# Selective scan: a second image by columns, whole products with C, sums two groups behind, softplus' parts added on TensorE, 11 of 32 products with B on GpSimd

## The chip, the cores and the metric

The kernel runs on one core of a Trainium2 chip. A core has five engines that run side by side and meet through semaphores: TensorE (PE in the profile: matmul), VectorE (DVE), ScalarE (ACT), GpSimd (POOL) and SyncE (SP, which issues most DMA here). SBUF is the working memory of 128 partitions, PSUM the memory that TensorE writes. The metric is the device time of one execution in microseconds, from the first to the last instruction and what lies around them; smaller is better.

## The reference

Four layers follow each other on an image of 2 x 128 channels x 64 x 64: attention (layer 0), a block with deformable convolutions (1), six 3 x 3 convolutions (2), and a selective scan in four directions (3). Only layer 3 is concerned:

```
x_norm = layernorm(x over channels);  x_norm_t = x_norm by columns
mamba(s):                                   # s: 4096 tokens of 128 channels, d_inner = 256
    xh, z = split(s @ W_in.T);  xh = silu(causal_conv4(xh) + conv_b)
    dt, B, C = split(xh @ W_xp.T)           # 8, 16, 16
    dt = softplus(dt @ W_dt.T + b_dt)
    dA = exp(dt * A);  dBu = dt * B * xh    # each 4096 x 256 x 16
    h_t = dA_t * h_(t-1) + dBu_t            # the scan
    y = sum_n h_t[n] * C_t[n] + xh * D;  return (y * silu(z)) @ W_out.T
out = x + fuse(mamba(x_norm), flip(mamba(flip)), and the same two of x_norm_t) + b_fuse
```

## The kernel before, in words

**Blocks, groups, slots.** Layer 3 walks through 64 blocks: two images, four directions (rows, columns, columns reversed, rows reversed), eight pieces of 512 tokens. A block has two halves of 128 inner channels, and a half has four groups of four states each (`NJ = 4`). A group is a tile `db` of 128 x 4 x 512: partition 32 j + c holds state j of the group and channel c, and the four columns q = 0..3 are the four sets of 32 channels. So a block has eight groups, called slots 0 to 7 here: slots 0 to 3 are the first half, 4 to 7 the second. Group k of the whole walk is slot k % 8 of block k // 8.

**A group's work.** `weights` spreads the group's four rows of B over the partitions with one matmul into PSUM (`pb`, two buffers of pool `psb`). `db_dve` (L1379) multiplies three of the four columns by B on VectorE, from PSUM; `db_pool` (L1386) does the fourth on GpSimd from a copy of B that DMA has spread in SBUF (`copies`). `expo` (L1393) makes exp(dt A) on ScalarE into one of three PSUM buffers. `scan` (L1402) runs the recurrence in place on VectorE, one column at a time. `keep` copies the last state, for two columns at a time, on ScalarE. `cmul` (L1413) multiplies by C in place on GpSimd, two columns at a time. `sums` (L1419, L1421) adds the states up on TensorE into `py`, of which there is one buffer; the first group of a half adds the D term first. After four groups `gate` (L1430) multiplies `py` by silu(z) on VectorE. `db` has four buffers.

**A block's preparation** goes on one block ahead, a piece in each slot: convolution (`conv`, one half in slot 6 and one in 7 of the block before), `conv_silu` in slot 0, the projections to dt, B and C (`xproj`, slot 1), `delta` and `softplus` (slots 2 and 3), the rest of B and C to full precision (`xproj_rest`, slot 4), silu(z) (slot 5). `softplus` is Relu(v) + ln(1 + exp(-|v|)); `spread` adds the parts and multiplies by u on GpSimd in slots 3 and 4, and the result goes to DRAM and back to have its channels spread over the partitions (`spread_store`, `spread_load`, on SP's queue). The finished block is projected (`project`, slot 3) and added to the image (`finish`, slot 4). The small PSUM tiles of all this share two buffers of pool `psm`.

**The order** is written out by hand: under `tc.manual_schedule()` each engine runs its instructions in program order, and a scheduler changes nothing. The loop over k runs, for each group: transfers, `weights(k+2)`, four times (an exponential two scans ahead, a scan), `db_dve(k+1)`, `db_pool(k+1)`, the products with C, the slot's piece of preparation, and `sums(k-1)` last. A step of iteration k on TensorE thus stands behind `weights(k+2)`, whose buffer is free when `db_dve(k)` has read it.

**Columns.** One normed image `xn` per image of the batch, by rows. The column directions read it with a stride (`window`), three halo rows on each side written by GpSimd. LN of image 1 runs during blocks 22 to 29, with its mean and variance in pool `psm`.

Of the kernel before, what the change touches and what calls it, by code (L numbers as in the profile page):

```python
# [10 lines left out]
F32 = mybir.dt.float32  # L11
# [1109 lines left out]
def layer3(g, I, out):  # L1121
# [7 lines left out]
    ND = 3  # L1129
    NNG = N_STATE // NJ  # L1130
    HB = 3
    with ExitStack() as ctx:
# [9 lines left out]
        wxp = a.tile([P, 2, 40], F32, name="wxp")  # L1142
        nc.sync.dma_start(wxp, I["wxpT"])
        wdt = a.tile([40, 2, P], F32, name="wdt")
        nc.sync.dma_start(wdt[32:40], I["wdtT"])
# [54 lines left out]
        xns = [a.tile([P, HW + 2 * HB, HW], F32, name=f"xn{b}") for b in range(NB)]  # L1200
# [3 lines left out]
        def ln_mean(b, k):  # L1204
            N[k, "mean"] = psm.tile([P, BLK], F32, name="pm3")
            nc.tensor.matmul(N[k, "mean"], onesm, interior(g, b, k * RB, RB), start=True, stop=True)
# [13 lines left out]
        def ln_var(b, k):  # L1220
            N[k, "var"] = psm.tile([P, BLK], F32, name="pm3")
            nc.tensor.matmul(N[k, "var"], onesm, N[k, "sq"], start=True, stop=True)
# [6 lines left out]

        def ln_store(b, k):  # L1230
            xn = xns[b]
            nc.scalar.activation(
                flat(xn[:, HB + k * RB : HB + (k + 1) * RB, :]), N[k, "xc"], AF.Identity, bias=vec(g, "ln_b"), scale=vec(g, "ln_w")
            )

        def columns_halo(b):

            xn = xns[b]
            top, bot = xn[:, 0:HB, :], xn[:, HB + HW :, :]
            nc.gpsimd.tensor_copy(top[:, :, 1:], xn[:, HW : HW + HB, : HW - 1])  # L1240
            nc.gpsimd.memset(top[:, :, 0:1], 0.0)
            nc.gpsimd.tensor_copy(bot[:, :, : HW - 1], xn[:, HB : 2 * HB, 1:])
            nc.gpsimd.memset(bot[:, :, HW - 1 :], 0.0)

        def rows_halo(b):
            nc.gpsimd.memset(xns[b][:, HB - 1, HW - HB :], 0.0)
            nc.gpsimd.memset(xns[b][:, HB + HW, :HB], 0.0)


        dirs = ((0, False, False), (2, True, False), (3, True, True), (1, False, True))  # L1250
# [4 lines left out]
            for c in (range(NBLK - 1, -1, -1) if dirs[nd][2] else range(NBLK))  # L1255
        ]
        NBK = len(blocks)
        S = {}

        def window(blk, shift):  # L1260

            b, nd, c = blk
            xn = xns[b]
            if dirs[nd][1]:
                r0 = HB - shift
                return xn[:, r0 : r0 + HW, c * RB : (c + 1) * RB].rearrange("p h w -> p w h")
            f0 = HB * HW + c * BLK - shift
            return flat(xn)[:, f0 : f0 + BLK]

        def shaped(blk, t):  # L1270

            return img(t) if dirs[blk[1]][1] else t

        def conv(i, hf):
            blk = blocks[i]
            sgn = -1 if dirs[blk[1]][2] else 1
            pu = S[i]["pu", hf] = psm.tile([P, BLK], F32, name="pm3")
            for s in range(4):
                nc.tensor.matmul(shaped(blk, pu), wcs[:, hf, s, :], window(blk, sgn * s), start=(s == 0), stop=(s == 3))  # L1279
# [7 lines left out]
        def zproj(i):  # L1287
            S[i]["pz"] = []
            for hf in range(2):
                pz = psm.tile([P, BLK], F32, name="pm3")  # L1290
                nc.tensor.matmul(shaped(blocks[i], pz), winz[:, hf, :], window(blocks[i], 0), start=True, stop=True)
# [8 lines left out]
        def xproj(i):  # L1300
            S[i]["px"] = px = psm.tile([P, BLK], F32, name="pm3")
            for hf in range(2):
                nc.tensor.matmul(px[:40, :], wxp[:, hf, :], S[i]["u"][:, hf, :], start=(hf == 0), stop=(hf == 1))

        def xproj_copy(i):

            px = S[i].pop("px")
            S[i]["xd"] = ck.tile([40, BLK], F32, name="xd", bufs=1)
            nc.scalar.copy(S[i]["xd"], px[:40, :])
# [17 lines left out]
        def delta(i, hf):  # L1327
            pdt = S[i]["pdt", hf] = psm.tile([P, BLK], F32, name="pm3")
            nc.tensor.matmul(pdt, wdt[32:40, hf, :], S[i]["xd"][32:40], start=True, stop=True)
# [9 lines left out]

        def spread(i, hf):  # L1340
            s_ = S[i]
            dd = s_["dd", hf]
            nc.gpsimd.tensor_add(dd[:, 0, :], dd[:, 0, :], dd[:, 1, :])
# [24 lines left out]
        def copies(i, x, ng):  # L1368

            t = S[i][x, ng] = ck.tile([P, BLK], F32, name=f"{x}4_{ng}", bufs=1)  # L1370
# [4 lines left out]
        def db_dve(k):  # L1375
            i, hf, ng = groups[k]
            x, n = G[k], ND
# [5 lines left out]
        def db_pool(k):  # L1383
            i, hf, ng = groups[k]
            x, n = G[k], ND
# [10 lines left out]
        def scan(k, q):  # L1396
            i, hf, ng = groups[k]
            d0, d1 = G[k].pop(("da", q)), G[k]["db"][:, q, :]
            if dirs[blocks[i][1]][2]:
# [4 lines left out]
        def keep(k, h):  # L1404
            i, hf, ng = groups[k]
            last = 0 if dirs[blocks[i][1]][2] else BLK - 1
            qs = slice(2 * h, 2 * h + 2)
            nc.scalar.copy(hl[:, hf, ng, qs], G[k]["db"][:, qs, last : last + 1])  # L1408

        def cmul(k, h):  # L1410
            i, hf, ng = groups[k]
            v = G[k]["db"][:, 2 * h : 2 * h + 2, :]
            nc.gpsimd.tensor_mul(v, v, S[i]["c", ng].unsqueeze(1).to_broadcast([P, 2, BLK]))  # L1413
# [18 lines left out]
        def project(i):  # L1432
# [4 lines left out]
            s_["xv"] = columns(g, b, c * RB, RB) if dirs[nd][1] else interior(g, b, c * RB, RB)  # L1437
            nc.tensor.matmul(img(pf), g.ident, s_["xv"], start=True, stop=False)
            for hf in range(2):
                nc.tensor.matmul(pf, mt[:, hf, dirs[nd][0], :], s_["gt", hf], start=False, stop=(hf == 1))  # L1440
# [16 lines left out]
        def begin(i):  # L1457
            if i < NBK:
                S[i] = {}
                if i % (4 * NBLK) in (0, 3 * NBLK):  # L1460
                    rows_halo(blocks[i][0])
                if i % (4 * NBLK) == NBLK:
                    columns_halo(blocks[i][0])
# [4 lines left out]
        def front_act(i, slot):  # L1468
            if i < NBK:
                if slot == 0:  # L1470
                    conv_silu(i)
                elif slot == 1:
                    xproj_copy(i)
                elif slot == 2:
                    softplus(i, 0)
                elif slot == 3:
                    softplus(i, 1)
                elif slot == 4:
                    rest_copy(i)
                elif slot == 5:  # L1480
                    zproj_silu(i)


        def transfers(i, slot):
            if i < NBK:
                if slot == 2:
# [13 lines left out]
        def front_pe(i, slot):  # L1500
            if i < NBK:
                if slot == 1:
# [267 lines left out]
```

## Time and profile before

| what | before |
|---|---|
| time, median of 3 runs | 5972.63 us (5970.81 to 5975.61) |
| the profiled execution's own time | 5970.06 us |
| its span, first to last instruction | 5968.2 us |
| first and last scan of layer 3 | about 2518 and 5955 us |
| VectorE, busy in the whole span | 4554.8 us (76%) |
| GpSimd | 3699.7 us (62%) |
| ScalarE | 3806.8 us (64%) |
| TensorE, matmul | 5213.9 us (87%) |
| mean granted TensorE clock | 0.899 |

The whole-span shares are means over stages. In the second half of the span, where the scan is, VectorE and GpSimd each show nine tenths or more in almost every slice. A matmul of 32-bit numbers shows as two instructions ("passes"), so the counts of TensorE's rows are twice those of the code. A matmul's duration in the profile is longer than its distance to the next one, since they are pipelined. "L1402" is line 1402 of the kernel before; "<-" in square brackets names what ended an engine's wait.

### The profile page before, as it was taken

How to read it: one execution, taken by the hardware profiler on the slowest of the kernel's cores; microseconds unless marked ns; L12 is line 12 of the kernel's file. 1: busy time of each engine (PE TensorE's matmuls, PEld its weight loads, DVE VectorE, ACT ScalarE, POOL GpSimd, SP SyncE). 2: the span in 40 equal slices, each digit the busy share in tenths (PEclk: the TensorE clock that was granted, in tenths of full speed). 3: DMA queues.
4: the chain of work that ended last, by engine and by line, in shares of the span. 5: the costliest groups of instructions: out<-in, count | busy, mean ns of one | idle time of the engine just before them, and what ended most of it. 6: DMA issues, size and time to landing. Idle time of an engine off the chain costs nothing.

```text
span 5968.2 us, 60083 instructions
## 1 busy us (share of the span) xinstructions
PE 5213.9 (87%) x18726; PEld 1661.8 (28%) x18726; DVE 4554.8 (76%) x4262; ACT 3806.8 (64%) x5867; POOL 3699.7 (62%) x2112
## 2 busy tenths in 40 slices
PE   7999999989978689877888988788878889888777
PEld 3333333334444234222222222222222222222221
DVE  5333333364134688599999999999999999999999
ACT  4888888830035411477777777777666777777765
POOL 5111111100010121299999999999999999999998
PEclk8999999999989899888888898878888898988887
DMA  5000001030066100255556555555566555655564
GB/s 153 18 18 18 19 18 33 1 58 1 15 117 114 46 4 0 55 144 133 136 135 149 139 137 132 141 138 134 144 146 145 133 137 133 150 140 135 134 147 106
DMA packets 357689, 575.61 MB, mean 96 GB/s; under 512 B 74696, under 2 KB 129360, under 8 KB 356272
## 3 DMA queue, kind: packets, MB, share of 16 engines
q1 hardware_dynamic: 354224, 568.13, 40.1%
q10 hardware_dynamic: 3136, 3.56, 0.2%
q8 instruction: 149, 2.44, 0.2%
q14 instruction: 180, 1.47, 0.1%
HBM read 482.34 MB, written 89.13 MB: 96 GB/s over the span
## 4 chain that ended last, share of the span: by engine, by line
DVE 46%; PE 39%; DMA 5%; issue 4%; POOL 3%; ACT 2%; SPq 1%; DVEq 0%; ACTq 0%; POOLq 0%
DVE db L1402 31%; DVE db L1379 11%; PE ps L287 10%; PE acc L303 8%; PE m L1052 5%; PE m L566 5%; PE acd L812 2%; DMA dd<-dx 2%; POOL db L1413 1%; PE m L526 1%; DVE gt L1430 1%; DMA b<-bx 1%; PE pf L775 1%; PE pm L1279 1%; PE py L1421 1%
## 5 line engine op out<-in xcount | busy, mean ns | idle before, releaser
L1413 POOL TENSOR_TENSOR db<-db,c 128x1024 f32<-128x1024 f32 x1024 | 2400.1, 2359 | 82.4 <-ACT hl L1408 72.8
L1402 DVE TENSOR_TENSOR_SCAN db<-da,hl,db 128x512 f32<-128x512 f32 x1792 | 2158.3, 1265 | 52.2 <-ACT da L1393 5.2
L1393 ACT ACTIVATE da<-dd,am 128x512 f32<-128x512 f32 x2048 | 1406.9, 689 | 901.9 <-DVE db L1402 895.1
L293 ACT ACTIVATE e<-ps 128x1024 f16<-128x1024 f32 x1024 | 992.2, 1021 | 134.6 <-PE ps L287 116.9
L1421 PE MATMUL py<-db,fold 128*32 128x512 f32 x4096 | 825.4, 680 | 195.9 <-POOL db L1413 195.6
L1379 DVE TENSOR_TENSOR db<-pbc,dd 128x1536 f32<-128x1536 f32 x512 | 889.0, 1736 | 1.8 <-DMA c<-bx 1.8
L1279 PE MATMUL pm<-xn,wcs 128*128 128x512 f32 x1024 | 723.1, 857 | 32.4 <-DVE xc L1217 19.3
L314 DVE RECIPROCAL rec<-acc 32x512 f32<-32x512 f32 x64 | 214.9, 3358 | 639.2 <-PE acc L303 612.0
L321 POOL TENSOR_TENSOR parts<-parts 32x512 f32<-32x512 f32 x64 | 80.4, 1256 | 975.1 <-DVE parts L320 975.1
L287 PE MATMUL ps<-q,k 32*128 32x512 f32 x4096 | 656.3, 643 | 3.5 <-DVE flag L250 2.7
L1386 POOL TENSOR_TENSOR db<-b,dd 128x512 f32<-128x512 f32 x512 | 650.9, 1271 | 4.2 <-DMA b<-bx 2.3
L303 PE MATMUL acc<-e,v 128*128 128x512 f16 x2048 | 531.4, 382 | 0.0
L1052 PE MATMUL m<-v,u 128*128 128x512 f32 x864 | 379.6, 603 | 49.4 <-DVE v L1021 49.4
L1419 PE MATMUL py<-u,ddp 128*128 128x512 f32 x256 | 178.1, 784 | 228.2 <-DVE gt L1430 227.9
L1365 PE MATMUL pbc<-bc,sel 64*128 64x512 f32 x512 | 283.9, 555 | 87.5 <-DVE db L1379 83.1
L1421 PEld LDWEIGHTS py<-db,fold 128*32 128x32 f32 x4096 | 115.2, 113 | 798.5 <-POOL db L1413 501.3
L1279 PEld LDWEIGHTS pm<-xn,wcs 128*128 128x128 f32 x1024 | 202.4, 209 | 426.9 <-issue 371.3
L1402 DVE TENSOR_TENSOR_SCAN db<-da,db 128x512 f32<-128x512 f32 x256 | 293.4, 1205 | 17.8 <-ACT da L1393 10.4
L303 PEld LDWEIGHTS <-v 128*128 128x128 bf16 x2048 | 158.4, 97 | 509.8 <-issue 388.4
L287 PEld LDWEIGHTS ps<-q,k 32*128 32x128 f32 x4096 | 229.6, 184 | 227.9 <-issue 145.1
L1365 PEld LDWEIGHTS pbc<-bc,sel 64*128 64x128 f32 x512 | 104.6, 204 | 603.9 <-DVE db L1379 310.1
L566 PE MATMUL m<-comb,w 64*128 64x512 f32 (+4 forms) x1296 | 269.9, 575 | 0.0
(311 smaller groups left out, 5734.7 us busy)
## 6 DMA issues: line engine op xcount, KB each, us to landing
dd<-dx SPq DMA_DIRECT2D x1024, 256.0 KB, 6.5
dx<-dd SPq DMA_DIRECT2D x128, 512.0 KB, 7.3
b<-bx SPq DMA_DIRECT2D x1024, 64.0 KB, 5.2
c<-bx SPq DMA_DIRECT2D x1024, 64.0 KB, 2.0
hats<-pos SPq DMA_DIRECT2D x136, 256.0 KB, 9.6
q<-qd SPq DMA_DIRECT2D x32, 512.0 KB, 8.4
w<-in_conv0T SPq DMA_DIRECT2D x18, 288.0 KB, 8.7
q<-in_x SPq DMA_DIRECT2D x8, 512.0 KB, 7.2
```

What stands on the lines that cost most here:

```text
L287: nc.tensor.matmul(ps[:, i, :], k4[h % 2][rows, kb // 4, :], q4[h % 2][rows, qb * BLK : (qb + 1) * BLK], start=True, stop=True,)
L293: nc.scalar.activation(e[:, :n, :], ps[:, :n, :], AF.Exp)
L303: nc.tensor.matmul(acc, v3[b][:, kb, h, :], e[:, i, :], start=(kb == 0), stop=(kb == NS - 1))
L566: yield lambda q=q, dy=dy, src=src, i0=i0, i1=i1: nc.tensor.matmul(m[:, i0 * NF : i1 * NF], w[half, dy, q, x, :], src, start=(dy == KC and ...
L1052: nc.tensor.matmul(m[x], weights[j][:, dy, x, :], v[j][b][:, x, r0 : r0 + RP, :].rearrange("p r i -> p (r i)"), start=(dy == 0), stop=(dy ...
L1279: nc.tensor.matmul(shaped(blk, pu), wcs[:, hf, s, :], window(blk, sgn * s), start=(s == 0), stop=(s == 3))
L1379: nc.vector.tensor_tensor(x["db"][:, :n, :], x.pop("pb").unsqueeze(1).to_broadcast([P, n, BLK]), S[i]["d4", hf][:, 1, :n, :], ALU.mult)
L1386: nc.gpsimd.tensor_tensor(x["db"][:, n:, :], S[i]["b", ng].unsqueeze(1).to_broadcast([P, 4 - n, BLK]), S[i]["d4", hf][:, 1, n:, :], ALU.mult)
L1393: nc.scalar.activation(da, S[i]["d4", hf][:, 0, q, :], AF.Exp, scale=am[:, hf, q, ng : ng + 1])
L1402: nc.vector.tensor_tensor_scan(d1, d0, d1, 0.0 if first else hl[:, hf, ng, q, :], ALU.mult, ALU.add)
L1413: nc.gpsimd.tensor_mul(v, v, S[i]["c", ng].unsqueeze(1).to_broadcast([P, 2, BLK]))
L1421: nc.tensor.matmul(S[i]["y", hf][32 * q : 32 * q + 32, :], fold, G[k]["db"][:, q, :], start=False, stop=(ng == NNG - 1),)
```

## The change

Seven edits in layer 3, with the sizes of PSUM and of `db` as before:

- Products with B: a table `ND[half][group]` says how many of the four columns VectorE does: 2, 4, 1, 4 in the first half and 1, 4, 1, 4 in the second. GpSimd does the rest, 11 of 32 (8 before). Groups with 4 need no copy of B by DMA.
- Products with C and the state copies are whole: one GpSimd instruction and one ScalarE instruction of four columns a group.
- `sums` runs for the group two behind, not one behind. The gates move from slots 5 and 1 (after the fourth scan) to slots 6 and 2 (after the second scan).
- The parts of softplus are added by TensorE (two matmuls with the identity) and copied back by ScalarE; GpSimd only multiplies. The weights for dt are laid out twice, so that both halves' `delta` stand in one slot.
- The preparation moves about one slot forward; `project` and `finish` stand in slot 5, with the first half's convolution behind them, and the second half's in slot 6; `conv_silu` is in slot 7.
- The image lies twice in SBUF: `xn` by rows and `xt` by columns, each serving both images of the batch. `turn` makes one from the other on ScalarE in slot 6 of a few blocks. Image 1 starts with the columns. The halo rows and their GpSimd copies go.
- LN takes its two PSUM tiles from pool `psb`, the one of `weights`, and runs in slots 0, 1, 3, 4 and 5 of blocks 22 to 29.

```diff
-    ND = 3
+    ND = ((2, 4, 1, 4), (1, 4, 1, 4))
...
-    HB = 3
+    HB = 1
+    HC = 3
...
-        wxp = a.tile([P, 2, 40], F32, name="wxp")
+        wxp = a.tile([P, 2, 72], F32, name="wxp")
...
-        xns = [a.tile([P, HW + 2 * HB, HW], F32, name=f"xn{b}") for b in range(NB)]
+        xn = a.tile([P, HW + 2 * HB, HW], F32, name="xn")
+        xt = a.tile([P, L + 2 * HC], F32, name="xt")
...
-            N[k, "mean"] = psm.tile([P, BLK], F32, name="pm3")
+            N[k, "mean"] = psb.tile([P, BLK], F32, name="pbc")
...
-            N[k, "var"] = psm.tile([P, BLK], F32, name="pm3")
+            N[k, "var"] = psb.tile([P, BLK], F32, name="pbc")
...
+        def turn(b, k):
+            if b:
+                nc.scalar.copy(by_row(k), by_column(k))
+            else:
+                nc.scalar.copy(by_column(k), by_row(k))
...
+        dirs = (
+            ((0, False, False), (2, True, False), (3, True, True), (1, False, True)),
+            ((2, True, False), (3, True, True), (0, False, False), (1, False, True)),
+        )
...
-            if dirs[nd][1]:
-                r0 = HB - shift
-                return xn[:, r0 : r0 + HW, c * RB : (c + 1) * RB].rearrange("p h w -> p w h")
-            f0 = HB * HW + c * BLK - shift
-            return flat(xn)[:, f0 : f0 + BLK]
+            f0 = c * BLK - shift
+            if dirs[b][nd][1]:
+                return xt[:, HC + f0 : HC + f0 + BLK]
+            return flat(xn)[:, HB * HW + f0 : HB * HW + f0 + BLK]
...
+        def sum_parts(i, hf):
+            ps = S[i]["dt", hf] = psm.tile([P, BLK], F32, name="pm3")
+            for x in range(2):
+                nc.tensor.matmul(ps, g.ident, S[i]["dd", hf][:, x, :], start=(x == 0), stop=(x == 1))
+
+        def sum_copy(i, hf):
+            nc.scalar.copy(S[i]["dd", hf][:, 0, :], S[i].pop(("dt", hf)))
...
-            nc.gpsimd.tensor_add(dd[:, 0, :], dd[:, 0, :], dd[:, 1, :])
...
+            if x == "b" and ND[0][ng] == ND[1][ng] == 4:
+                return
...
-            x, n = G[k], ND
+            x, n = G[k], ND[hf][ng]
...
-            nc.scalar.copy(hl[:, hf, ng, qs], G[k]["db"][:, qs, last : last + 1])
+            nc.scalar.copy(hl[:, hf, ng], G[k]["db"][:, :, last : last + 1])
...
-            v = G[k]["db"][:, 2 * h : 2 * h + 2, :]
-            nc.gpsimd.tensor_mul(v, v, S[i]["c", ng].unsqueeze(1).to_broadcast([P, 2, BLK]))
+            v = G[k]["db"]
+            nc.gpsimd.tensor_mul(v, v, S[i]["c", ng].unsqueeze(1).to_broadcast([P, 4, BLK]))
...
                 if slot == 0:
-                    conv_silu(i)
+                    xproj_copy(i)
                 elif slot == 1:
-                    xproj_copy(i)
+                    softplus(i, 0)
                 elif slot == 2:
-                    softplus(i, 0)
+                    softplus(i, 1)
+                    sum_copy(i, 0)
                 elif slot == 3:
-                    softplus(i, 1)
+                    sum_copy(i, 1)
+                    rest_copy(i)
                 elif slot == 4:
-                    rest_copy(i)
-                elif slot == 5:
                     zproj_silu(i)
+            if i + 1 < NBK and slot == 7:
+                conv_silu(i + 1)
...
-                if slot == 2:
+                if slot == 1:
                     bc_store(i)
...
-                if slot == 1:
+                if slot == 0:
                     xproj(i)
+                elif slot == 1:
+                    delta(i, 0)
+                    delta(i, 1)
                 elif slot == 2:
-                    delta(i, 0)
+                    sum_parts(i, 0)
                 elif slot == 3:
-                    delta(i, 1)
+                    sum_parts(i, 1)
+                    xproj_rest(i)
                 elif slot == 4:
-                    xproj_rest(i)
-                elif slot == 5:
                     zproj(i)
             if i + 1 < NBK:
-                if slot == 6:
+                if slot == 5:
                     begin(i + 1)
-                elif slot == 7:
+                elif slot == 6:
                     conv(i + 1, 1)
...
-        LN = {6: ln_mean, 7: ln_square, 8: ln_var, 9: ln_scale, 10: ln_store}
+        LN = {0: ln_mean, 1: ln_square, 3: ln_var, 4: ln_scale, 5: ln_store}
...
-                    for j, hf in (((k - 5) // 8, 0), ((k - 9) // 8, 1)):
-                        if q == 3 and 8 * j + 5 + 4 * hf == k and 0 <= j < NBK:
+                    for j, hf in (((k - 6) // 8, 0), ((k - 10) // 8, 1)):
+                        if q == 1 and 8 * j + 6 + 4 * hf == k and 0 <= j < NBK:
                             gate(j, hf)
-
-                    if q == 2 and live:
-                        keep(k, 0)
                 if more:
                     db_dve(k + 1)
                     db_pool(k + 1)
                 if ended:
-                    cmul(k - 1, 1)
+                    cmul(k - 1)
+                if i >= 1 and i <= NBK:
+                    if slot == 5:
+                        project(i - 1)
+                        finish(i - 1)
                 front_pe(i + 1, slot)
                 front_act(i + 1, slot)
                 front_pool(i + 1, slot)
-                if i >= 1 and i <= NBK:
-                    if slot == 3:
-                        project(i - 1)
-                    elif slot == 4:
-                        finish(i - 1)
                 if live:
                     next_norm(i, slot)
-                if live:
-                    cmul(k, 0)
-                if ended:
-                    sums(k - 1)
+
+                    if slot == 6 and i % (4 * NBLK) < NBLK // 2:
+                        for n in range(2):
+                            turn(blocks[i][0], 2 * (i % (4 * NBLK)) + n)
+
+                if 0 <= k - 2 < len(groups):
+                    sums(k - 2)
```

## The prediction

> **What bounds the kernel now.** I read the page's busy table and slices, then layer 3 (the scan, the only part that changes) by stretches, by groups and in order of time. Four rows of the costliest groups carry the stage:
>
> ```profile
> L1413 POOL TENSOR_TENSOR db<-db,c 128x1024 f32<-128x1024 f32 x1024 | 2400.1, 2359 | 82.4 <-ACT hl L1408 72.8
> L1402 DVE TENSOR_TENSOR_SCAN db<-da,hl,db 128x512 f32<-128x512 f32 x1792 | 2158.3, 1265 | 52.2 <-ACT da L1393 5.2
> ...
> L1379 DVE TENSOR_TENSOR db<-pbc,dd 128x1536 f32<-128x1536 f32 x512 | 889.0, 1736 | 1.8 <-DMA c<-bx 1.8
> ...
> L1386 POOL TENSOR_TENSOR db<-b,dd 128x512 f32<-128x512 f32 x512 | 650.9, 1271 | 4.2 <-DMA b<-bx 2.3
> ```
>
> Busy time by stretches (eight blocks in this row; columns: length, then PE, PEld, DVE, ACT, POOL, granted clock, DMA share, GB/s):
>
> ```profile
> 4235.00:4664.00 429.00, 351.55 (x918) 92.38 (x917) 420.84 (x337) 301.37 (x543) 417.44 (x229) 0.84 0.58 141
> ```
>
> VectorE is busy 420.8 of 429 us and GpSimd 417.4: two engines at once. The scan runs from 2518 to 5955 us, 53.7 us for each of 64 blocks. The waits of VectorE there come to some 10 us, 8.3 of them for ScalarE's exponentials. So VectorE's order sets the time, and GpSimd has about 1 us a block to spare.
>
> The clock decides what TensorE can do in a gap. In order of time, TensorE's instructions from a block start to a projection, and one convolution:
>
> ```profile
> 4366.79 1.92 PE L1421 MATMUL py<-db,fold 128*32 128x512 f32 x4 [1.66 <-POOL db L1413]
> 4368.78 0.79 PE L1365 MATMUL pbc<-bc,sel 64*128 64x512 f32 x1
> 4369.50 2.07 PE L1329 MATMUL pm<-xd,wdt 8*128 8x512 f32 x2
> 4371.50 2.08 PE L1438 MATMUL pm<-xa,ident 128*128 128x512 f32 x2
> 4373.37 3.36 PE L1440 MATMUL pm<-gt,mt 128*128 128x512 f32 x4
> 4376.66 1.07 PE L1421 MATMUL py<-db,fold 128*32 128x512 f32 x8
> ...
> 4397.76 3.70 PE L1279 MATMUL pm<-xn,wcs 128*128 128x512 f32 x8
> ```
>
> A 512-column pass costs 0.43 us from start to start when fast (the next instruction after the convolution starts 3.64 us on) and 0.85 when slow; projecting took 5.16 us, almost all slow. And where the order is tight already, on ScalarE:
>
> ```profile
> 4352.16 0.69 ACT L1393 ACTIVATE da<-dd,am 128x512 f32<-128x512 f32 x1 [0.37 <-DVE db L1402]
> 4352.87 1.28 ACT L1284 ACT_TABLE_LOAD   x1
> 4354.16 1.26 ACT L1284 ACTIVATE u<-pm,vecs 128x512 f32<-128x512 f32 x2
> 4355.44 1.28 ACT L1285 ACT_TABLE_LOAD   x1
> 4356.74 0.69 ACT L1393 ACTIVATE da<-dd,am 128x512 f32<-128x512 f32 x1
> ```
>
> The last exponential ends at 4357.43; its scan, the third of a group whose scans began at 4355.05, starts at 4357.45. This place has no slack.
>
> **What the skill says.** "TensorE: Matmul & The Clock Gate", What's actually happening: an idle window of about 3.4 us halves the clock, and a busy one frees it. The trace agrees in kind: 0.43 and 0.85 us, slow after waits. "PSUM — Partial Sum Buffer", Engine vs sequencer instructions: matmuls start and complete in program order, so one that waits holds back all behind it. "GPSIMD Engine Reference", Elementwise — side-by-side cycle accounting: 4497 ns for a two-input f32 operation of 2048 elements; two halves at 2359 less one overhead give 4.53 here.
>
> **The change, part by part.** D5 is the start of slot 5's first scan, and so on.
>
> VectorE's products with B: a block had 8 of three tiles, now 4 of four, 1 of two and 3 of one. The slope is (1736 - 666)/2 = 535 ns a tile, with the gate (512, also from PSUM, 666 ns) as the second point. Before 8 x 1.736 = 13.89; after 4 x 2.271 + 1.201 + 3 x 0.666 = 12.28. It saves 1.61 us a block, 103 over 64.
>
> GpSimd: products with C 8 x 4.53 = 36.3 in place of 37.5; products with B one of two tiles (2.36) and three of three (2359 + 1088 = 3447 ns), 12.7 in place of 10.2; the sum of softplus' parts goes, -2.55. It comes to 51.4 a block against 52.7, under VectorE's 52.05 (53.65 pure before, less 1.6). A product with C cannot start before all four scans and the state copy, yet two iterations pass until its sums are wanted. I followed GpSimd through a block, each product with C from the state copy (1.2 to 4.4 us after the last scan, by what ScalarE does in that slot): its products with B end 1.3 to 4.8 us before the scan that wants them. So this costs nothing, hidden by VectorE's scans; without that cover up to 2 us in four groups, 8 a block.
>
> DMA: 512 of 1024 copies of B go; the store of B and C moves one slot forward in SP's queue, ahead of a copy of C. That queue has waits of its own for GpSimd (860 us), so nothing is priced. ScalarE: eight state copies of 0.18 us fewer, two sum copies of about 0.58, 16 image turns of 0.7 to 1.2 in all: in its waits for VectorE.
>
> TensorE: the sum of softplus' parts is two matmuls for each half, eight passes, 3.4 to 6.8 us a block in slots 2 and 3, where TensorE waits for VectorE anyway. Slow, it delays the second rest matmul of slot 3 and ScalarE's copy of it: 8.3 us after D3, then 0.57 and 0.67, against a scan due at 7.9, up to 1.6 lost; fast, it is done at 4.3. I take 0 and leave 0 to 0.4 a block in the range. The parts' path: product 1.27, store 7.3, eight loads issued in 3.3, landing 6.5: 18.4 us from the start of slot 4, wanted some 22 us on by slot 7's third scan. Hidden by three slots of scans.
>
> Slot 7: the convolution's silu moves from slot 0 to 7. The product behind the scans is now of two tiles, not three, so the third scan of the next group comes 0.535 us sooner against the same 3.9 us of table loads and silus. VectorE stalls 0.55 a block: +35 us. Before the softplus (2.43 us in slots 1 and 2) there is still 0.4.
>
> Slot 5, the heart. TensorE now has, in this order: weights, projection, a half convolution, and the last sums of the first half; the gate that reads them stands after the second scan of slot 6. The weights wait for the buffer of slot 5's product, free at D5. The gate is due four scans (4.73), a product of one tile (0.76) and two scans (2.40) later: 7.9 us. Fast: weights 0.42, image 0.86, projection 1.72, convolution 3.63, sums 1.06 = 7.7, so no stall. Where the image is read by columns its pass is 0.94 to 1.04 at either clock: 8.7 to 8.9, stall 1.0. Slow until the convolution: 0.72 + 1.87 + 3.29 + 3.63 + 1.06 = 10.6, stall 2.7; slow into the convolution, 4. Which? Ahead of D5, TensorE ends slot 4's sums and idles about 3.7 us, until slot 5's product is read. Of five idle times of 3 us before the first matmul of a half (2716, 2770, 2824, 2877, 4387), the passes after were slow for 0 to 3.6 us, in one case 6. Half of that is lost: 0 to 3. I take 1.5, bounds 0.3 and 3.3: +96 us (19 to 211). Making the convolution contiguous for columns (1037 against 593 ns in the median) is what lets it take 3.63 in every block; alone it gains nothing, since nothing waited for it.
>
> LN of image 1 (eight blocks). Mean and variance move to the two buffers of the weights. The mean in slot 0 takes the buffer of slot 1's product and waits until D1; the weights of slot 1 then wait until D2 rather than D1, and hold back softplus' first matmul. From D2: 0.4 to 0.7, then 0.86 to 1.7, softplus 2.43, the square 0.63, an exponential 0.67: 5.0 to 6.1, where the scan wanted it at 3.1: 1.9 to 3.0 lost. The variance in slot 3 shifts slot 4 the same way: the gates' matmul waits until D5, then two silus, a table load, the logarithm and the root stand ahead of the exponential: 3.7 to 5.5. I take 7 of 5.6 to 8.5: 8 x 7 = +56 (45 to 68).
>
> The end: the last product is whole, 2.2 later, and two sums follow: +3.
>
> Against the profiled execution's own 5970: 5970 - 103 + 35 + 96 + 56 + 3 = 6057. The median of the runs shown is 2.6 above the profiled one: 6060.
>
> **The rivals.** *TensorE in time* (ends on the other side): it runs fast from D5 and LN's waits fall in slack: 5970 - 103 + 35 + 3 = 5905. For it: the new additions fill idle time in slots 2 and 3. Against: 3.7 us of idle just ahead. It decides below 0.15 us of stall at the gate if LN costs 56, below 1.0 if nothing. *Fast clock only*: rows 0, columns 1.0 in 32 blocks, LN 45: 5970 - 103 + 35 + 32 + 45 + 3 = 5982. *Slow throughout*: 64 x 3.3 + 68: 5970 - 103 + 35 + 211 + 68 + 3 = 6184. For it: before, the projection's passes had a median of 1.06 us in most row stretches. *GpSimd becomes the bound*: it starts each product late and slides to 54.5 a block: 64 x 0.85 = +54, 6025. Against: its own sum is 51.4.
>
> **How the numbers follow.** The likeliest, a mixed clock, 0.53, own range 6000 to 6120; slow throughout 0.15; TensorE in time 0.14; fast clock only 0.12; GpSimd 0.06. From 5950 to 6170 I leave out most of the 5905 case and half of the slow one, near 0.2. A measurement tells no change from about 0.2% (12 us). Faster 0.13, the fast rival but for a small part; same 0.08, most of "fast clock only"; slower 0.79.
>
> **What would show it.** The product from PSUM at 2.27, 1.20 and 0.67 us; GpSimd's whole product near 4.5. VectorE's waits: gate <- sums as the longest, about 100 us over 64 times, all in slot 6; scan <- exponential about 0.5 us once a block, and larger in eight blocks from 3700 to 4150 us. GpSimd below 97% with waits for the state copy. It is wrong if the gate never waits (TensorE fast at D5), if GpSimd leads VectorE's waits, or if the eight LN blocks are as long as the others.

## The result, and the profile after

The changed kernel takes 6112.5 us (median of 4, 6106.84 to 6114.27) against 5972.3 for the kernel before on the same chip: a ratio of 1.0233, with a 95% interval from 1.022 to 1.0245. It is slower by 140 us; 87 were forecast. Every time below is the median of four executions; one of the last run's four took 8536 us, and its figures are of the other three. The profiled execution has a span of 6112.2 us (5968.2 before) and a mean granted clock of 0.874 (0.899).

The rows of the costliest groups that answer to those of before (last part: the idle time of the engine just ahead of the group, and what ended it):

```profile
L1430 POOL TENSOR_TENSOR db<-db,c 128x2048 f32<-128x2048 f32 x512 | 2313.4, 4528 | 110.5 <-ACT hl L1425 103.1
L1420 DVE TENSOR_TENSOR_SCAN db<-da,hl,db 128x512 f32<-128x512 f32 x1792 | 2171.8, 1265 | 128.6 <-ACT da L1411 79.3
...
L1404 POOL TENSOR_TENSOR db<-b,dd 128x1536 f32<-128x1536 f32 (+1 forms) x256 | 810.7, 3167 | 152.8 <-DMA c<-bx 84.1
L1395 DVE TENSOR_TENSOR db<-pbc,dd 128x2048 f32<-128x2048 f32 (+2 forms) x512 | 783.0, 1529 | 3.5 <-DMA b<-bx 3.5
```

VectorE's products with B cost 783 us, 106 less than before; the scans cost what they did (1265 ns each). The work fell, and the idle time ahead of it grew. The waits of VectorE from 2600 to 6080 us (in all, how often, the longest):

```profile
DVE gt L1447 <- PE py L1438: 132.6, 69, 3.3
DVE db L1420 <- ACT da L1411: 90.5, 77, 6.0
DVE db L1420 <- POOL db L1404: 2.7, 7, 0.7
```

The gate waits for the sums, and scans for exponentials; GpSimd is hardly waited for. The stretch of the eight LN blocks, first before, then after (columns as in the prediction: length, PE, PEld, DVE, ACT, POOL, clock, DMA share, GB/s):

```profile
3696.50:4134.00 437.50, 355.53 (x947) 99.26 (x945) 426.23 (x345) 315.54 (x570) 421.40 (x233) 0.83 0.56 137
```

```profile
3731.20:4246.80 515.60, 374.88 (x1017) 111.53 (x1017) 417.07 (x344) 324.06 (x529) 418.32 (x121) 0.79 0.46 110
```

VectorE is busy 417 us against 426, but the eight blocks last 516 us in place of 437.5. No engine is full in them: here all wait for each other in turn.

I went through VectorE's instructions in order of time and added up each idle time by the slot in which it falls. This closes the account from the first scan to the last:

| where | forecast | measured |
|---|---|---|
| products with B | -103 | -106 (2263, 1196 and 662 ns) |
| slot 0, third scan waits for ScalarE | +35 | +36 (0.56 to 0.68 in each of 62 blocks) |
| slot 6, gate waits for the sums | +96 | +122.7 (61 blocks) |
| LN blocks, slots 2 and 5 | +56 | +68 |
| rest | | +4 |
| first scan to last scan | | +125 (3562 against 3437) |
| ahead of the first scan | 0 | +16.5 |
| after the last scan | +3 | +2 |

### The profile page after: what moved, and what is told of

Read it like the earlier page. It is cut to its first block, busy times and chain, and to the rows that moved or that the text cites. A ratio compares the mean times of both kernels' runs of the same rounds, so it can differ in the third digit from the quotient of the medians.

```text
span 6112.2 us, 58645 instructions
## 1 busy us (share of the span) xinstructions
PE 5030.6 (82%) x19238; PEld 1760.2 (29%) x19238; DVE 4461.1 (73%) x4266; ACT 3821.3 (63%) x5499; POOL 3632.8 (59%) x1200
## 4 chain that ended last, share of the span: by engine, by line
PE 47%; DVE 35%; ACT 9%; issue 5%; DMA 2%; POOL 1%; SPq 1%; DVEq 0%; POOLq 0%; ACTq 0%
DVE db L1420 22%; PE ps L287 10%; DVE db L1395 10%; PE acc L303 8%; PE m L1052 5%; PE m L566 4%; PE pm L1285 3%; PE pm L1457 3%; ACT da L1411 2%; PE pm L1455 2%; PE pm L1350 2%; PE acd L812 2%; ACT L1291 1%; ACT L1290 1%; ACT u L1290 1%
## 5 line engine op out<-in xcount | busy, mean ns | idle before, releaser
L1430 POOL TENSOR_TENSOR db<-db,c 128x2048 f32<-128x2048 f32 x512 | 2313.4, 4528 | 110.5 <-ACT hl L1425 103.1
L1420 DVE TENSOR_TENSOR_SCAN db<-da,hl,db 128x512 f32<-128x512 f32 x1792 | 2171.8, 1265 | 128.6 <-ACT da L1411 79.3
L1379 PE MATMUL pbc<-bc,sel 64*128 64x512 f32 x512 | 300.8, 587 | 802.1 <-DVE db L1395 787.6
L1404 POOL TENSOR_TENSOR db<-b,dd 128x1536 f32<-128x1536 f32 (+1 forms) x256 | 810.7, 3167 | 152.8 <-DMA c<-bx 84.1
L1395 DVE TENSOR_TENSOR db<-pbc,dd 128x2048 f32<-128x2048 f32 (+2 forms) x512 | 783.0, 1529 | 3.5 <-DMA b<-bx 3.5
L1438 PE MATMUL py<-db,fold 128*32 128x512 f32 x4096 | 617.8, 679 | 14.1 <-POOL db L1430 14.1
L1350 PE MATMUL pm<-dd,ident 128*128 128x512 f32 x512 | 361.7, 845 | 3.3 <-ACT dd L1343 3.1
L686 POOL TENSOR_SCALAR yt<-y 32x512 f32<-32x512 f32 x8 | 18.2, 2271 | 380.3 <-DVE y L677 379.9
L1285 PE MATMUL pm<-xn,wcs 128*128 128x512 f32 x512 | 237.1, 606 | 6.5 <-ACT xn L1243 3.7
L1052 PEld LDWEIGHTS m<-v,u 128*128 128x128 f32 x864 | 166.9, 194 | 262.0 <-issue 215.5
```

The costliest lines, as they stand in the source:

```text
L1052: nc.tensor.matmul(m[x], weights[j][:, dy, x, :], v[j][b][:, x, r0 : r0 + RP, :].rearrange("p r i -> p (r i)"), start=(dy == 0), stop=(dy ...
L1350: nc.tensor.matmul(ps, g.ident, S[i]["dd", hf][:, x, :], start=(x == 0), stop=(x == 1))
L1395: nc.vector.tensor_tensor(x["db"][:, :n, :], x.pop("pb").unsqueeze(1).to_broadcast([P, n, BLK]), S[i]["d4", hf][:, 1, :n, :], ALU.mult)
L1404: nc.gpsimd.tensor_tensor(x["db"][:, n:, :], S[i]["b", ng].unsqueeze(1).to_broadcast([P, 4 - n, BLK]), S[i]["d4", hf][:, 1, n:, :], ALU.mult)
L1420: nc.vector.tensor_tensor_scan(d1, d0, d1, 0.0 if first else hl[:, hf, ng, q, :], ALU.mult, ALU.add)
L1438: nc.tensor.matmul(S[i]["y", hf][32 * q : 32 * q + 32, :], fold, G[k]["db"][:, q, :], start=False, stop=(ng == NNG - 1),)
```

## The gate's wait

Slot 5 of a row block on TensorE, and VectorE's gate behind it, in order of time (start, length, what, and in brackets the idle time ahead):

```profile
5367.32 1.06 PE L1438 MATMUL py<-db,fold 128*32 128x512 f32 x8
5372.05 0.49 PE L1379 MATMUL pbc<-bc,sel 64*128 64x512 f32 x1 [3.66 <-DVE db L1395]
5372.47 1.25 PE L1455 MATMUL pm<-xa,ident 128*128 128x512 f32 x2
5373.51 3.50 PE L1457 MATMUL pm<-gt,mt 128*128 128x512 f32 x4
5376.85 3.60 PE L1285 MATMUL pm<-xn,wcs 128*128 128x512 f32 x8
5380.38 1.06 PE L1438 MATMUL py<-db,fold 128*32 128x512 f32 x8
```

```profile
5372.10 4.81 DVE L1420 TENSOR_TENSOR_SCAN db<-da,hl,db 128x512 f32<-128x512 f32 x4
5376.82 0.66 DVE L1395 TENSOR_TENSOR db<-pbc,dd 128x512 f32<-128x512 f32 x1
5377.59 2.46 DVE L1420 TENSOR_TENSOR_SCAN db<-da,hl,db 128x512 f32<-128x512 f32 x2
5381.51 0.69 DVE L1447 TENSOR_TENSOR gt<-py,z 128x512 f32<-128x512 f32 x1 [1.46 <-PE py L1438]
```

The order is that of the prediction: weights, projection, half a convolution, and only then the sums, whose inputs GpSimd had finished 8 us earlier (at 5372.17). After 3.66 us of idling the projection takes 3.34 us from start to start, where a fast one takes 1.72; the convolution behind it is fast again (3.53). Over the blocks the medians after are 1.85 for the image and 3.16 for the projection by rows, 1.98 and 2.74 by columns. Typical waits of the gate are 1.46 by rows and 1.8 by columns; the first two blocks of each later direction wait 2.3 to 3.1, and the eight LN blocks 20.2 us in all.

**The order alone.** The sums of slot 5 are issued ahead of the projection and the convolution; nothing else changes.

```diff
+                if slot == 5 and 0 <= k - 2 < len(groups):
+                    sums(k - 2)
                 if i >= 1 and i <= NBK:
                     if slot == 5:
                         project(i - 1)
...
-                if 0 <= k - 2 < len(groups):
+                if slot != 5 and 0 <= k - 2 < len(groups):
                     sums(k - 2)
```

> In slot 5 alone, the sums of the group two behind are issued right behind the weights, ahead of the projection and the convolution; nothing else moves. Theory (the gate waits for TensorE's order in slot 5): the gate's wait in slot 6, 122.7 us over 61 blocks, falls to under 10. The projection ends 1.1 us later, and ScalarE's addition to the image behind it, so up to 0.5 us a block may come back as a wait of slot 6's third scan: 5990 to 6030 us, ratio to before 1.003 to 1.010. Rival (sums are late because whole products with C end late on GpSimd): the gate still waits 100 us or more, and the time stays above 6090. Rival (the slow clock alone delays the sums, wherever they stand): half of the wait stays, about 6050.

Measured: 6004.0 us, ratio 1.0051 (1.0034 to 1.0068), 108 us less than the changed kernel. VectorE's waits, over the same stretch:

```profile
DVE db L1420 <- ACT da L1411: 114.9, 108, 5.9
DVE gt L1447 <- PE py L1438: 10.1, 5, 6.9
```

All of slot 6's 122.7 us of waits for the sums is gone. In its place are 25 us, in slot 6 of 32 blocks (in 22 of them the image is read by columns), where a scan waits for its exponential: the projection now ends about 2 us later, ScalarE's `finish` waits for it, and the exponentials stand behind `finish`. The waits in slot 0 are as they were, and those in slots 2 and 5 of the LN blocks fall from 68 to 61. So the place of the sums is what the gate's 123 us hang on.

**The clock alone.** TensorE is given work during its idle time at the end of slot 4: slot 6's product of the weights, several times over into the buffer that it fills anyway. First seven times, then fifteen.

```diff
+                if slot == 4 and k + 2 < len(groups):
+                    ii, _, ng2 = groups[k + 2]
+                    for _ in range(7):          # 15 in the second run
+                        nc.tensor.matmul(
+                            G[k + 2]["pb"], sel[:, ng2].rearrange("p j c -> p (j c)"), S[ii]["bc"], start=True, stop=True
+                        )
```

> At the end of slot 4, where TensorE sits idle for 3.7 us, the weights' matmul of slot 6 is issued seven times more into the same tile (3 us of work at the fast rate; the result is the same). Slot 5's order is as in the changed kernel. Theory (the order sets 7.7 us by rows and about 8.8 by columns against a gate due at 7.9, and a slow clock adds the rest): the projection's passes turn fast, 0.43 us apart; by rows the gate's wait of 1.46 falls to under 0.2, by columns 1.8 to about 0.9; 122.7 us in all become 30 to 45, time 6025 to 6045. Rival (the order alone, the clock does not matter): the wait stays at 1.5 or grows, since more work stands ahead: 6112 or more. Rival (GpSimd is late): no change, 6112.

Measured: 6084.1 us, ratio 1.0185 (1.0168 to 1.0202): a miss. The seven matmuls took only 1.89 us, so 1.85 us of idling was left, and the projection was still slow (median 2.47 by rows). The gate waited 94 us. That is too little work to decide anything, hence the second run:

> As the run with seven repeats, but fifteen: seven took 1.9 us and left 1.85 us of idle time ahead of slot 5, after which the projection was still slow in part; fifteen at the same pace fill some 3.5 of the 3.7 us. Theory (order 7.7 us by rows and 8.8 by columns, the clock the rest): the projection's four passes take about 1.8 us in place of 2.5 to 3.2, the gate's wait by rows falls from 1.4 to under 0.3 and by columns from 1.8 to 0.3 to 0.9; in all 20 to 40 us in place of 93.9 with seven and 122.7 without: 6020 to 6045. Rival (the clock has its own rhythm and does not follow this work): the wait stays near 94, 6080.

Measured: 6043.1 us, ratio 1.0115 (1.0098 to 1.0132), 69 us less than the changed kernel. The same slot on TensorE:

```profile
5322.65 3.77 PE L1634 MATMUL pbc<-bc,sel 64*128 64x512 f32 x15
5326.38 0.49 PE L1379 MATMUL pbc<-bc,sel 64*128 64x512 f32 x1
5326.81 1.13 PE L1455 MATMUL pm<-xa,ident 128*128 128x512 f32 x2
5327.77 1.88 PE L1457 MATMUL pm<-gt,mt 128*128 128x512 f32 x4
5329.49 3.60 PE L1285 MATMUL pm<-xn,wcs 128*128 128x512 f32 x8
```

With the idle time filled, the projection takes 1.71 to 1.74 us in 61 of 63 blocks. From the start of the weights to the convolution it is now 3.10 us by rows and 4.14 by columns; in the changed kernel it was 4.80 and 5.14 in the median, and in 28 of 29 row blocks 1.5 to 2.9 us more than 3.10. Both differences are found again in the gate's wait: row blocks lose theirs wholly, and column blocks keep 0.8 us, which is the image read with a stride (1.98 us for two passes, unchanged). Slot 6 keeps 54.5 us of waits, but 26 of them lie in the eight LN blocks, which had 20 in the changed kernel. In the other 56 blocks the wait falls from 102 to 28 us: 74 us come from the slow clock after TensorE's idling, and the rest from what precedes the sums even at the fast clock. That rest is the "fast clock only" case of the prediction, which put 1.0 us on each column block.

**Sums one group behind, as before.** Both gates go back to their old places too.

```diff
-                    for j, hf in (((k - 6) // 8, 0), ((k - 10) // 8, 1)):
-                        if q == 1 and 8 * j + 6 + 4 * hf == k and 0 <= j < NBK:
+                    for j, hf in (((k - 5) // 8, 0), ((k - 9) // 8, 1)):
+                        if q == 3 and 8 * j + 5 + 4 * hf == k and 0 <= j < NBK:
                             gate(j, hf)
...
-                if 0 <= k - 2 < len(groups):
-                    sums(k - 2)
+                if ended:
+                    sums(k - 1)
```

> The sums one group behind and the gates in slots 5 and 1 after the fourth scan, as before the change; whole products with C and all else as changed. Theory: the first half's sums then stand in slot 4, ahead of the projection, so the gate no longer waits 122.7 us for the order of slot 5; but TensorE now waits for each whole product on GpSimd, 4.5 us from its start, and its next preparation and ScalarE behind it come late: more than 100 us of TensorE's waits for GpSimd return and some of them reach VectorE through ScalarE: 6000 to 6090. Rival (sums two behind are what costs): 5990 or less.

Measured: 6033.5 us (6025.7 to 6045.6), ratio 1.0104 (1.0087 to 1.0122). The gate in slot 5 waits 26 us over 34 blocks, in place of 123 over 61. LN's waits stay (5.4 to 6.0 us in slot 5 and 2.4 to 3.7 in slot 2, a block), and slot 0's 36. The sums two groups behind, in the place that they were given, cost 79 us net: the time that the second group gave them was spent on the projection and the convolution ahead of them.

## LN, slot 0 and the products with C

**LN elsewhere.** LN of image 1 takes its two PSUM tiles from `psm` again, those of image 0 go to the buffers of the exponentials, and the steps of image 1 are spread so that the variance, the logarithm and the root stand ahead of the silu of slot 4.

```diff
-            N[k, "mean"] = psb.tile([P, BLK], F32, name="pbc")
+            N[k, "mean"] = psm.tile([P, BLK], F32, name="pm3") if b else psd.tile([P, BLK], F32, name="da")
...
-            N[k, "var"] = psb.tile([P, BLK], F32, name="pbc")
+            N[k, "var"] = psm.tile([P, BLK], F32, name="pm3") if b else psd.tile([P, BLK], F32, name="da")
...
+        LN1 = {7: ln_mean, 8: ln_square, 12: ln_scale, 13: ln_store}
+        LN1_EARLY = {12: (ln_var, ln_root)}
...
+                if live:
+                    next_norm(i, slot, True)
                 front_pe(i + 1, slot)
                 front_act(i + 1, slot)
```

> LN no longer takes tiles from the weights' pool: image 0 uses the three buffers of the exponentials (idle then), image 1 uses the small tiles' pool, with its mean in slot 7 of the block before, its variance ahead of slot 4's matmuls and the root ahead of slot 4's silu. Theory (a weights tile taken in slot 0 and slot 3 shifts TensorE by an iteration): in blocks 22 to 29 the waits in slots 2 (1.4 and 1.1 us) and 5 (5.8 us) go, but for 0.5 us in slot 5: 65 us less; the first scan comes about 10 us sooner (2535 before); the gate's wait in slot 6 stays at 1.5 to 2.3. Time 6030 to 6045. Rival (LN's own work on ScalarE and VectorE makes the eight blocks long): 20 us less at most.

Measured: 6025.0 us, ratio 1.0085 (1.0069 to 1.0102), 88 us less than the changed kernel and some 5 better than expected. It splits into three: LN's own waits fall from 68 us to 4, the gate's in slot 6 from 122.7 to 110 (all of it in the LN blocks, from 20.2 to 5.9), and the first scan starts at 2523.8 in place of 2534.6. In the changed kernel an LN block looks so on VectorE and on TensorE:

```profile
3961.32 2.46 DVE L1420 TENSOR_TENSOR_SCAN db<-da,hl,db 128x512 f32<-128x512 f32 x2
3969.67 2.46 DVE L1420 TENSOR_TENSOR_SCAN db<-da,hl,db 128x512 f32<-128x512 f32 x2 [5.89 <-ACT da L1411]
```

```profile
3961.27 0.79 PE L1379 MATMUL pbc<-bc,sel 64*128 64x512 f32 x1 [4.97 <-DVE db L1395]
3961.99 3.78 PE L1297 MATMUL pm<-xn,winz 128*128 128x512 f32 x4
```

TensorE idles 4.97 us until slot 5's product frees a buffer, runs silu(z)'s matmuls at the slow clock (3.78 us), and ScalarE holds silu, table load, logarithm and root ahead of the exponential that the third scan wants: 5.89 us lost, where the prediction had 3.7 to 5.5.

The start is the same edit's doing. The first LN mean on TensorE, before the change and after it, with what stands ahead:

```profile
2453.29 3.75 PE L1206 MATMUL pm<-xa,onesm 128*128 128x512 f32 x4 [11.08 <-DVE onesm L1149]
```

```profile
2459.05 3.75 PE L1164 MATMUL pbc<-wfu,wout 128*128 128x512 f32 x4 [16.38 <-DMA wfu<-in_wfuseT]
2462.59 0.64 PE L1174 MATMUL pbc<-ident,ws 128*128 128x128 f32 x2
...
2465.25 2.08 PE L1212 MATMUL pbc<-xa,onesm 128*128 128x512 f32 x2
```

The preparation of the weights uses pool `psb` as well; with LN in that pool, the first mean stands behind a matmul that waits for a DMA, 12 us later than before. Moving image 0's tiles away gives 10.8 of the 16.5 us back. The first scan's time differs between executions, mostly by what comes ahead of layer 3, but the groups stay apart: 2529.0 to 2538.1 in seven runs with these tiles in `psb`, 2520.9 to 2527.7 in four with them moved. In the changed kernel the rest of the start has block 1's silu and its two table loads ahead of the first exponential (from 2530.00 to 2533.87), where before they stood behind a scan; that this is what is left was not tried alone.

**Slot 0's stall.** The split of the products with B in the first half becomes 3, 4, 1, 3 in place of 2, 4, 1, 4.

```diff
-    ND = ((2, 4, 1, 4), (1, 4, 1, 4))
+    ND = ((3, 4, 1, 3), (1, 4, 1, 4))
```

> The share of products with B alone: the first half's groups get 3, 4, 1, 3 columns on VectorE in place of 2, 4, 1, 4, so 21 of 32 as in the changed kernel, but three ahead of slot 0. Theory (slot 0's third scan waits 0.56 us a block because the product ahead of it is shorter than ScalarE's table loads and silus): that wait goes, 36 us over 64 blocks, and VectorE's own work stays: 6070 to 6085. Rival (the wait is ScalarE's, whatever stands on VectorE): no change.

Measured: 6101.6 us, ratio 1.0216 (1.0199 to 1.0233): 11 us gained, where about 36 were expected. Slot 0's stall did go, from 36 us to nothing. But the gate's wait rose by 23, from 122.7 to 145.9. TensorE again, a row block:

```profile
5406.42 1.06 PE L1438 MATMUL py<-db,fold 128*32 128x512 f32 x8 [0.97 <-POOL db L1430]
5410.12 0.79 PE L1379 MATMUL pbc<-bc,sel 64*128 64x512 f32 x1 [2.64 <-DVE db L1395]
5410.84 2.07 PE L1455 MATMUL pm<-xa,ident 128*128 128x512 f32 x2
5412.70 3.37 PE L1457 MATMUL pm<-gt,mt 128*128 128x512 f32 x4
```

From the weights to the convolution it is 5.72 us by rows, against 4.80, and 5.77 by columns, against 5.14; the typical wait of the gate is 2.37 against 1.46, and 2.4 against 1.8. The two differences agree: most of what VectorE saved in slot 0, it waited for in slot 6, because the same matmuls ran at a slower clock; another 7 us there are waits for GpSimd. That happened though the idle time just ahead was shorter (2.64 against 3.66); here it is broken by a wait of 0.97 for GpSimd's product. Why the clock was slower then is not settled. This split also needs copies of B for the fourth group again (768 in place of 512).

**Products with C in halves again**, and the state copies with them, each half behind its two scans:

```diff
-            v = G[k]["db"]
-            nc.gpsimd.tensor_mul(v, v, S[i]["c", ng].unsqueeze(1).to_broadcast([P, 4, BLK]))
+            v = G[k]["db"][:, 2 * h : 2 * h + 2, :]
+            nc.gpsimd.tensor_mul(v, v, S[i]["c", ng].unsqueeze(1).to_broadcast([P, 2, BLK]))
```

> Products with C and state copies in halves again, as before the change, all else as changed. Theory (whole products cost nothing, GpSimd's lateness reaches no scan): within 15 us of the changed kernel's 6112; GpSimd has 1.2 us a block more to do. Rival (whole products start too late and hold the sums): the gate's wait falls by half or more, 6050 or less.

Measured: 6108.7 us, ratio 1.0227 (1.021 to 1.0244), no different from the changed kernel within the interval. Between 2600 and 6080 us the gates waited 113.5 us in place of 132.6, and the scans 19.1 for GpSimd in place of 2.7: one was exchanged for the other, nearly all of it in slot 6 of the eight LN blocks. That a whole product waits for all four scans cost nothing in this kernel, as forecast.

## The parts together

**Three mendings**: the sums of slot 5 first, with `finish` moved behind the first exponential of slot 6; LN elsewhere; and the split 3, 4, 1, 3.

```diff
+                    if q == 0 and slot == 6 and 1 <= i <= NBK:
+                        finish(i - 1)
...
+                if slot == 5 and 0 <= k - 2 < len(groups):
+                    sums(k - 2)
                 if i >= 1 and i <= NBK:
                     if slot == 5:
                         project(i - 1)
-                        finish(i - 1)
```

> The changed kernel with the four causes taken away together: sums first in slot 5; the addition to the image behind slot 6's first exponential (so that the later projection does not hold it); LN's tiles elsewhere; 3, 4, 1, 3 columns. Theory: 122.7 (gate) + 36 (slot 0) + 68 (LN) + 11 (start) us go, 4 come back: 6112 - 234 = 5878, between 5865 and 5905, ratio to before 0.982 to 0.989. If a wait on GpSimd or TensorE takes their place, above 5930.

Measured: 5945.4 us, ratio 0.9955 (0.9938 to 0.9971): faster than both kernels, but far from the 5878 expected. VectorE's waits:

```profile
DVE db L1423 <- POOL db L1407: 48.9, 52, 2.5
DVE db L1423 <- ACT da L1414: 20.1, 33, 1.0
DVE gt L1450 <- PE py L1441: 6.9, 1, 6.9
```

The longest is now GpSimd, at slot 6's second scan, the first that takes a product with B from it. A stretch of row blocks:

```profile
5220.00:5660.00 440.00, 336.39 (x1022) 103.38 (x1015) 425.21 (x349) 308.79 (x513) 425.18 (x126) 0.84 0.58 139
```

VectorE is busy 425.2 us of 440 and GpSimd just as long. GpSimd's gaps, 15 us here, are all in one place, just ahead of its product with B for the next block's slot 0:

```profile
5234.21 3.70 PE L1288 MATMUL pm<-xn,wcs 128*128 128x512 f32 x8
5237.75 1.02 PE L1439 MATMUL py<-u,ddp 128*128 128x512 f32 x2
5238.70 1.06 PE L1441 MATMUL py<-db,fold 128*32 128x512 f32 x8
```

```profile
5239.93 1.28 POOL L1407 TENSOR_TENSOR db<-b,dd 128x512 f32<-128x512 f32 x1 [1.25 <-DMA c<-bx]
```

The product starts 0.17 us after slot 6's sums have ended, and so it does in 57 of 63 blocks, whatever the trace names as the releaser: the four `db` buffers go round in turn, so these sums read the one that the product is going to fill, and they stand behind half a convolution. GpSimd loses 118 us in this way over the run and then works almost without a gap up to slot 6's product, for which VectorE waits 49 us in all. So TensorE's order may be behind this wait too; slot 6's sums ahead of the convolution were not tried.

The next two runs ask whether it is GpSimd's total that holds VectorE back, or the place of one product.

```diff
-    ND = ((3, 4, 1, 3), (1, 4, 1, 4))
+    ND = ((2, 4, 1, 4), (1, 4, 1, 4))     # first run; the second has (3, 4, 1, 4) for the first half
```

> The run with all three mendings, but with the split of the products with B as the change has it (slot 0 two on VectorE, slot 3 all four). If GpSimd was what held that run back (51.7 us of instructions in a block of 52.5, 49 us of waits of slot 6's first scan for its product with B), nothing is gained or lost by much here, since GpSimd has the same eleven products: the stall of 0.56 us in slot 0 comes back (+36 at most) and takes the wait for GpSimd away (-49 at most): 5925 to 5955 us. If only the new split of slot 3 was at fault (one product more on GpSimd just there), the wait for GpSimd goes without another: 5905 to 5920 us.

Measured: 5928.5 us, ratio 0.9928 (0.9911 to 0.9944). Slot 0's stall is back (36 us) and the waits for GpSimd fell to 7.7, within the range expected if GpSimd's total sets the pace: a stall elsewhere gives it the time. But the run is 17 us faster than the one before with the same eleven products, done in one instruction a block fewer (10 us of GpSimd's work over the scan). So their number alone does not set the time; their place counts too.

> The run with all three mendings, but with ten products with B of 32 on GpSimd instead of eleven (slot 0 three on VectorE, slot 3 all four). If GpSimd's work sets the block there: 64 products of 1.28 us less on GpSimd (-82 us of its work), 64 times 0.54 us more on VectorE (+34), the waits for GpSimd (49 us) mostly gone: 5925 to 5935 us, with under 15 us of waits of scans for GpSimd. If the waits came from a late copy of B or from the order of work, and not from GpSimd's total, they stay and VectorE's work is added: 5965 to 5985 us.

Measured: 5906.7 us, ratio 0.9887 (0.9867 to 0.9907), some 18 us better than expected. VectorE's waits are down to

```profile
DVE gt L1450 <- PE py L1441: 6.9, 1, 6.9
DVE db L1423 <- ACT da L1414: 5.4, 10, 0.7
DVE db L1423 <- POOL db L1407: 0.6, 1, 0.6
```

and the row stretch, in the columns of the stretches above, reads

```profile
5220.00:5660.00 440.00, 352.45 (x1034) 106.66 (x1034) 432.63 (x354) 315.50 (x523) 418.37 (x117) 0.82 0.54 128
```

VectorE is busy 98% here, and from the first scan to the end it waits for others for 14 us. With ten products on GpSimd, this version takes 67 us less than the kernel before and 206 less than the changed one. The run differs from the first of the three in one product that left GpSimd in slot 3, and so in its total and its place at once; the two are not told apart. It differs from the second in a product of slot 0, which costs VectorE about what slot 0's stall had cost. The work that the change saves VectorE is thus real: with the change's own split the kernel is 46 us faster than before, once TensorE's order and LN's buffers no longer give the saving back.

## Why the prediction was right, and where not

- **Direction and mechanism: right.** The likeliest case, a mixed clock, held: the gate behind the sums is the longest wait, 123 of its 133 us in slot 6, and GpSimd does not lead. The rivals "TensorE in time" and "fast clock only" are out, since the gate waits in 61 blocks, those by rows too; "slow throughout" (211 us at the gate) and "GpSimd the bound" also. The time lies near the upper end of the mixed case's own range, 6000 to 6120.
- **Products with B: right** (2.26, 1.20 and 0.66 us against 2.27, 1.20 and 0.67). **GpSimd's whole product: right** at 4.53, and its start behind four scans cost nothing, which the run with halves showed for this kernel.
- **Slot 0: right**, 0.56 us a block against 0.55.
- **The gate: mechanism right, size off.** The term was 1.5 us in 64 blocks; it measured 122.7 us in 61, 2.0 each, within the bounds of 0.3 and 3.3. What was mis-sized is one term, "I take 1.5", for every block. The typical row block did wait 1.46. The typical column block waited 1.8, because 1.0 from the slow clock came on top of the 0.8 that stays when TensorE does not idle (1.0 in the prediction); the first two blocks of a later direction waited up to 3.1, and the LN blocks 2.5 in the mean.
- **LN: size off**, 68 us in place of 56, at the bound of 45 to 68. Slot 5 lost 5.7 to 6.0 us where 3.7 to 5.5 were allowed; the trace has silu(z)'s passes all slow there. Slot 2 kept to its 1.9 to 3.0 (2.8 in the typical block). The prediction had no term for LN in slot 6, where moving its tiles took 14 us off the gate's wait. With them, LN cost some 78 us (64 in slots 2 and 5, and 14), above its bound.
- **The start: missed**, 16.5 us. The prediction followed LN's move to `psb` for image 1 alone. The same move puts image 0's first mean behind the weights' preparation; moving these tiles gave 10.8 us back, and the rest stays open.
- **Slot 3's rest matmul: right** at nothing.

The misses, by the place where they show, are 27 us at the gate, 12 in LN's slots and 16.5 at the start. They make up 55 of the 57 us by which the sum of 6057 fell short of the profiled execution's own time, 6114.0.

## What to carry to other kernels

A consumer of a result late in TensorE's order waits for all that was issued ahead of it: put the sums that another engine is waiting for first, and the work that nobody waits for behind them. When tiles move to another buffer pool, follow every use of that pool, the start of the kernel included. And when one wait goes, ask what comes next in line: here GpSimd's lateness showed only once three other waits were gone. Work for an engine that stalls anyway can be free: one product of 32 moved into slot 0's stall on VectorE, and the kernel was 22 us faster.

## What was not expected of the hardware

Repeating the same small matmul (64 x 128 weights, operands in the rounded 32-bit type) took about 0.25 us each (15 in 3.77 us, 7 in 1.89), where a single one takes 0.42 from its start to the next. And an idle time that is shorter, but in two pieces (0.97 and 2.64 us in place of one of 3.66), went with slower matmuls after it, not faster ones.
